# Three bursts of scores in each half batch in place of four, and both value products at the end of odd half batches

## The chip, the cores and the metric

The kernel runs on one core of one Trainium2 chip, all in float32. The metric is the device time of one execution in microseconds. Three runs of the kernel before took 1550.56, 1550.92 and 1552.35 us, so the median is 1550.92 us.

The core's engines are named as the profile names them: TensorE (PE; its weight loads are PEld), VectorE (DVE), ScalarE (ACT), GpSimd (POOL), and SyncE (SP), which here only issues DMAs. [...]

## The reference

The model is one layer: cross-attention of 64 queries over 1601 context keys in 32 batches, then a small attention over the 64 rows with a score that depends on positions, then a feed-forward part with a shared expert and two experts for each row. The cross-attention, cut to what matters:

```python
qh = _split_heads(q @ wq_w.T + wq_b)          # 32 batches, 16 heads of 16, 64 queries
kh = _split_heads(k @ wk_w.T + wk_b)          # 1601 keys
vh = _split_heads(v @ wv_w.T + wv_b)
scores = jnp.einsum('bhqd,bhkd->bhqk', qh, kh) / jnp.sqrt(jnp.float32(D_K))
scores = jnp.where(mask, scores, jnp.float32(-1000000000.0))
attn = jax.nn.softmax(scores, axis=-1)
out = jnp.einsum('bhqk,bhkd->bhqd', attn, vh)
```

The second attention ("span") takes 512 rows of 256 further: `mean = sigmoid(span0) * m`, `soft = softplus(span1)`, `scores = -soft * (pos - mean)**2`, softmax, and a product with the values. Here one tile of it holds 128 rows, that is two batches.

## The kernel before

**Tiling.** The keys of a batch are 13 blocks of 124, the last one padded. The work goes by half batches: half batch n = (b, c) holds batch b and heads 8c to 8c+7, as four pairs of heads j = 0 to 3. There are 64 half batches. For each, `scores` multiplies the transposed keys `kT` by the block-diagonal queries `qbd`. The four pairs j sit in four strips of 32 rows of TensorE, so the four products of one block run side by side, each into its own PSUM bank (psc). VectorE adds the mask (L510) and writes the sum to `prob`; it also takes a running maximum over blocks (`maximum`, L531), block by block, into `mrun` and, with the last block, into `mx`. `turned_maxima` transposes mx on TensorE (pm, L538), `maxima_of_rows` reduces it on VectorE (mc, L545), `maxima_along_rows` spreads it again (pb on TensorE, L553, and the copy mb on ScalarE, L557). GpSimd then subtracts mb from the four pairs (`less_maxima`, L562), ScalarE takes the exponentials (L567), and `values` (pvs, L577) multiplies them with the values, in two calls r = 0 and 1 of two pairs each, in strips of 32 columns.

**Pipeline.** In the step of the main loop for half batch n, the scores of n + 1, a part of the keys (`project_keys`, pk, L456) and values (`project_values`, pv) of batch b + 1, the subtraction and exponentials of n and the value products of n - 1 are all interleaved. The order is written out: a manual schedule holds TensorE, VectorE, ScalarE and GpSimd to the order in which the program issues their instructions; SyncE is left out of it. A key or value projection that is marked tiled also goes in strips of 32 columns; others use the whole array.

**Stretches.** A step of the loop has four stretches g = 0 to 3, one for each burst of scores, for blocks 0-3, 4-6, 7-9 and 10-12 (`GROUPS`); `BETWEEN` says which maxima VectorE takes in each. The context comes in the same four pieces. Into stretch g the loop puts the scores of burst g, the keys of piece g, a unit of values (two blocks), the subtraction of pair g, and the exponential of pair g - 1. The exponential of pair 3 and `values(n - 1, 0)` stand at the start of the next step, and `values(n - 1, 1)` in stretch 0, behind pb.

**The agenda.** What belongs to a tile of two batches is written as generators (`query_steps`, `span_steps`) whose pieces `run(stretch)` puts at the end of a stretch; `WAITS` says how many stretches lie between two pieces (`CLOSE` for the last two tiles). `finish_steps` transposes and divides the value products of a finished batch. The pieces of span_steps, in order: (0) po, the residual and its mean; (1) its normalisation; (2) its transpose tr_h; (3) psp, span and z; (4) an exponential; (5) sixteen small operations on VectorE; (6) a GpSimd subtraction on sc; (7) a square and a GpSimd product on sc; (8) a minimum on VectorE; (9-12) exponentials on ScalarE in four parts; (13) a reciprocal and a GpSimd product on sc; (14) pval; (15) eight transposes psa; (16) po2 (L339); (17) po3 (L349), the residual, its mean and the store x_kept; (18) a normalisation; (19) the transpose tr_f.

**PSUM.** Six banks are shared in turn by everything but two (`mm_bank`): psc, pm, pk, pb, pv and the tiles' products. A new use takes a bank that an earlier user has been read out of. One bank holds pvs and, in its other half, the transposed pvs; one holds mrun.

Of the kernel before, what the change touches and what calls it, by code (L numbers as in the profile page):

```python
# [20 lines left out]
PSUM = bass.MemoryType.PSUM  # L21

# [11 lines left out]
BETWEEN = [(), (1, 2, 3), (4, 5, 6), (7, 8, 9), (10, 11, 12)]  # L34
# [42 lines left out]
def perceiver_kernel(ctx: ExitStack, tc: tile.TileContext, a: dict[str, bass.AP], out: bass.AP):  # L77
# [34 lines left out]
    def load_x(t: int):  # L112
        xs[t] = work.tile([P, D], F32, tag="x", bufs=4, name=f"x{t}")
        nc.sync.dma_start(out=xs[t], in_=a["x"][t * P : (t + 1) * P, :])
# [98 lines left out]
    WAITS = (1, 1, 1, 1, 6, 1, 1, 1, 1, 1, 1, 1, 1, 3, 1, 3, 1, 1, 1)  # L213
    CLOSE = (1, 1, 1, 1, 2, 1, 1, 1, 1, 0, 0, 0, 1, 1, 1, 1, 1, 1, 1)

    SMALL = 5

    def waits_of(t: int):
        return CLOSE if t >= NTILE - 2 else WAITS

    def span_steps(t: int, oT):
        waits = iter(waits_of(t))
# [154 lines left out]


# [6 lines left out]
    def pair_of(n: int, j: int):  # L385
        return prob[:CHUNK, place(n, j // 2), j % 2]
# [15 lines left out]
    nc.vector.memset(pvs, 0.0)  # L402

# [89 lines left out]
    def scores(n: int, g: int, between=(), then=None):  # L493

        b, c = halves[n]
        c0, nb = GROUPS[g]
        pss = [mm_bank(f"psc_{b}_{c}_{g}_{j}") for j in range(4)]
        for k in range(nb):
            for j, ps in enumerate(pss):
                at = (c0 + k) * CHUNK  # L500
                nc.tensor.matmul(  # L501
                    ps[:CHUNK, k * P : (k + 1) * P],
                    lhsT=kTs[c][32 * j : 32 * j + 32, at : at + CHUNK],
                    rhs=qbd[b // 2][32 * j : 32 * j + 32, c, b % 2, :, :],
                    start=True, stop=True, tile_position=(32 * j, 0),
                )
        between = deque(between)
        held = then() if then else None
        for j, ps in enumerate(pss):
            nc.vector.tensor_tensor(  # L510
                pair_of(n, j)[:, c0 : c0 + nb, :].rearrange("p k (e q) -> p k e q", e=2),
                ps[:CHUNK, : nb * P].rearrange("p (k e q) -> p k e q", k=nb, e=2),
                madd[:CHUNK, c0 : c0 + nb, None, :].to_broadcast([CHUNK, nb, 2, S]), ALU.add,
            )
            if between and j:
                maximum(n, between.popleft())
            if j == 1 and held is not None:
                maxima_of_rows(*held)
# [127 lines left out]
    def finish_steps(b: int, stretch: int):  # L646
# [14 lines left out]
        if b % 2:  # L661
            agenda[stretch + 1].append(span_steps(t, oT.pop(t)))
            held_at.add(stretch + 1 + sum(waits_of(t)[:SMALL]))
# [19 lines left out]
    for g in range(len(GROUPS)):  # L683
        scores(0, g, BETWEEN[g])
        if g == 0:
            first_maxima(0)
        project_keys(0, 1, g)
    for k in BETWEEN[-1]:
        maximum(0, k)
# [13 lines left out]
    extra = {4 * last - 4: (0,), 4 * last - 3: (1, 2), 4 * last - 2: (4, 5), 4 * last - 1: (6,)}  # L703
    for n, (b, c) in enumerate(halves[:-1]):
        if c == 0 and b + 1 < B:
            load_context(b + 1)
        if c and b % 2 == 0 and b // 2 + 1 < NTILE:
            agenda[4 * n + 2].append(query_steps(b // 2 + 1))
# [4 lines left out]

        if n:
            values(n - 1, 0)
            exponentials(n - 1, 3)
        for g in range(len(GROUPS)):
            if g == 0:
                turned = []

                def turn():
                    turned.extend(turned_maxima(n))
                    return turned

                scores(n + 1, g, BETWEEN[g], turn)
                project(project_keys, c, 0)
                m = maxima_along_rows(turned[1])
                less_maxima(n, 0, m, nc.gpsimd)
                if 4 * n not in held_at:
                    first_maxima(n + 1)  # L730
                run(4 * n)
                if n:
                    values(n - 1, 1)
                    if c == 0:
                        agenda[4 * n + 1].append(finish_steps(b - 1, 4 * n + 1))
            else:
                scores(n + 1, g, BETWEEN[g])
                project(project_keys, c, g, g == 3)
                if g == 1:
                    project(project_values, 3 * c)  # L740
                elif g == 2:
                    project(project_values, 3 * c + 1)
                else:
                    for u in (5, 6) if c else (2,):
                        project(project_values, u, True)
            if g == 3:
                for k in BETWEEN[-1]:
                    maximum(n + 1, k)
            if g:
                less_maxima(n, g, m, nc.gpsimd)  # L750
                run(4 * n + g)
            for u in extra.get(4 * n + g, ()):
                linear_factor(u)
            if g == 0:
                if 4 * n in held_at:
                    first_maxima(n + 1)
            else:
                exponentials(n, g - 1)


    stretch = 4 * last
# [173 lines left out]
```

## Time and profile before

The profiled execution took 1550.89 us, and the span from its first to its last instruction is 1549.1 us; the clock granted to TensorE was 0.997.

| engine | busy us | share of the span |
|---|---|---|
| TensorE (PE) | 1494.5 | 96% |
| VectorE (DVE) | 1207.5 | 78% |
| GpSimd (POOL) | 1117.2 | 72% |
| ScalarE (ACT) | 953.1 | 62% |
| DMA engines | | 16% (two data queues: 15.5% and 0.2%) |

| work | count | mean ns of one | busy us |
|---|---|---|---|
| scores psc, L501 | 6656 | 284 | 263.4 |
| keys pk, L456 | 1768 | 498 | 404.0 |
| values pv, L456 | 3524 | 379 | 390.9 |
| value products pvs, L577 | 13312 | 220 | 216.4 |
| mask additions of 3 blocks, L510 | 768 | 547 | 404.3 |
| mask additions of 4 blocks, L510 | 256 | 681 | 163.8 |
| running maxima, L531 (without mx) | 704 | 687 | 483.4 |
| subtraction, L562 on GpSimd | 252 | 3741 | 938.9 |
| exponentials, L567 on ScalarE | 256 | 1588 | 403.2 |

A row of the timeline gives the start in us, the length in us, the engine, the line, the operation, output<-inputs, the shape, and in brackets the idle time of the engine before it and who ended it. Matmuls overlap, and a row's length takes in the way through the engine; what one group costs is best read from its start to the start of the next. A row for a matmul counts two instructions for each float32 product.

### The profile page before, as it was taken

To read this page: it belongs to the slowest core of one execution; us is meant where nothing else is said; L and a number is where in the kernel's file an instruction comes from. 1 tells how busy PE (TensorE), PEld (TensorE's weight loads), DVE (VectorE), ACT (ScalarE), POOL (GpSimd) and SP (SyncE) were. 2 spreads that over 40 slices of the span, in tenths; PEclk is the share of its full clock that TensorE was granted. 3 is DMA by queue.
4 is the path that set the end of the run, shared out by engine and by line. 5 is a ranking of instruction groups with operands and counts; after the bars stand their busy time and mean duration, and the time that the engine had idled before them with its cause. 6 is when DMAs were issued, how large, how long until landed. Compare 5 with 4: busy or idle time off the path is not lost.

```text
span 1549.1 us, 61567 instructions
## 1 busy us (share of the span) xinstructions
PE 1494.5 (96%) x27856; PEld 1090.3 (70%) x27856; DVE 1207.5 (78%) x2460; ACT 953.1 (62%) x1725; POOL 1117.2 (72%) x506
## 2 busy tenths in 40 slices
PE   8999999999999999999999999999999999988999
PEld 5677767677777777676767767676777677654587
DVE  4888988878798888888888988888788988884100
ACT  3565676766667666766667566766666676757511
POOL 1777787887778787888777887878877787872610
PEclk9999999999999999999999999999999999999999
DMA  5111111111111111111111111111111111005100
GB/s 169 53 45 44 37 45 36 42 45 52 45 52 46 39 35 39 45 39 51 46 52 46 52 32 42 35 39 48 45 52 45 52 41 33 9 3 161 58 28 28
DMA packets 52070, 73.71 MB, mean 48 GB/s; under 512 B 3812, under 2 KB 51040, under 8 KB 51680
## 3 DMA queue, kind: packets, MB, share of 16 engines
q1 hardware_dynamic: 50992, 69.00, 15.5%
q8 instruction: 218, 3.57, 0.9%
q10 hardware_dynamic: 816, 0.79, 0.2%
q14 instruction: 44, 0.36, 0.1%
HBM read 65.57 MB, written 4.19 MB: 45 GB/s over the span
## 4 chain that ended last, share of the span: by engine, by line
PE 58%; POOL 18%; DVE 18%; ACT 4%; issue 2%; DMA 1%; ACTq 0%; POOLq 0%; DVEq 0%
PE pk L456 14%; POOL prob L562 13%; PE pv L456 12%; PE psc L501 9%; DVE mrun L531 8%; PE pvs L577 8%; DVE prob L510 6%; PE py L865 4%; PE u L606 3%; PE pm L538 2%; PE ph L847 2%; ACT prob L567 2%; POOL sc L289 2%; POOL sc L284 2%; PE pb L553 1%
## 5 line engine op out<-in xcount | busy, mean ns | idle before, releaser
L562 POOL TENSOR_TENSOR prob<-prob,mb 124x1664 f32<-124x1664 f32 x252 | 938.9, 3741 | 270.1 <-ACT mb L557 259.2
L510 DVE TENSOR_TENSOR prob<-psc,madd 124x384 f32<-124x384 f32 (+1 forms) x1024 | 568.1, 580 | 188.8 <-PE psc L501 187.5
L531 DVE TENSOR_TENSOR mrun<-prob,mrun 124x512 f32<-124x512 f32 x704 | 483.4, 687 | 4.4
L567 ACT ACTIVATE prob<-prob 124x1664 f32<-124x1664 f32 x256 | 403.2, 1588 | 44.5 <-POOL prob L562 41.4
L456 PE MATMUL pk<-ct,wkT_sb 128*32 128x361 f32 (+2 forms) x1768 | 404.0, 498 | 7.5 <-DMA wkT_sb<-in_wkT 5.5
L456 PE MATMUL pv<-wvT_sb,ct 128*124 128x256 f32 x3524 | 390.9, 379 | 0.0
L456 PEld LDWEIGHTS pv<-wvT_sb,ct 128*124 128x124 f32 x3524 | 273.4, 132 | 120.1 <-issue 16.3
L501 PE MATMUL psc<-qbd,kT 32*124 32x128 f32 x6656 | 263.4, 284 | 4.5 <-issue 2.3
L471 ACT ACTIVATE kT<-pk,cols 128x372 f32<-128x372 f32 (+2 forms) x256 | 151.6, 592 | 183.3 <-PE pk L456 182.5
L501 PEld LDWEIGHTS psc<-qbd,kT 32*124 32x124 f32 x6656 | 212.5, 181 | 55.2 <-DVE mrun L531 22.8
L488 ACT COPY v<-pv 124x512 f32<-124x512 f32 (+1 forms) x224 | 124.6, 556 | 198.3 <-PE pv L456 198.2
L456 PEld LDWEIGHTS pk<-ct,wkT_sb 128*32 128x32 f32 (+1 forms) x1768 | 158.2, 144 | 116.3 <-issue 51.5
L577 PE MATMUL pvs<-prob,v 124*17 124x64 f32 x13312 | 216.4, 220 | 12.0 <-ACT prob L567 10.3
L577 PEld LDWEIGHTS pvs<-prob,v 124*17 124x17 f32 x13312 | 197.2, 98 | 36.2 <-ACT prob L567 12.7
L296 ACT ACTIVATE sc<-sc,least 128x64 f32<-128x64 f32 x256 | 85.8, 340 | 0.0
L867 DVE SCALAR_TENSOR_TENSOR ot<-py,prob 128x256 f32<-128x256 f32 x16 | 6.8, 424 | 75.7 <-PE py L865 75.7
L523 ACT COPY mrun<-prob 124x512 f32<-124x512 f32 x64 | 38.4, 600 | 40.9 <-DVE soft L279 37.9
L606 PE MATMUL u<-xfT,sw_sb 128*128 128x512 f32 x128 | 57.6, 600 | 0.4 <-ACT xfT L360 0.4
L538 PE MATMUL pm<-cst,mx 124*128 124x124 f32 x256 | 41.1, 282 | 17.3 <-DVE mx L531 16.5
L553 PEld LDWEIGHTS pb<-cst,mc 128*124 128x124 f32 x256 | 29.0, 134 | 39.8 <-DVE mc L545 31.5
L296 ACT ACTIVATION_READ_ACCUMULATOR sc<-sc,least 128x1 f32 x256 | 48.8, 191 | 0.0
L854 ACT ACTIVATE hT<-ph,cols 128x256 f32<-128x256 f32 x32 | 13.4, 470 | 56.3 <-PE ph L847 56.3
(120 smaller groups left out, 1117.0 us busy)
## 6 DMA issues: line engine op xcount, KB each, us to landing
ct<-in_ctxT SPq DMA_DIRECT2D x64, 372.0 KB, 3.2
ct<-in_ctxT SPq DMA_DIRECT2D x32, 496.0 KB, 3.6
ct<-in_ctxT SPq DMA_DIRECT2D x32, 361.0 KB, 3.2
w<-in_w SPq DMA_DIRECT2D x16, 256.0 KB, 6.9
x<-in_x SPq DMA_DIRECT2D x16, 128.0 KB, 2.4
x_kept<-x SPq DMA_DIRECT2D x16, 128.0 KB, 1.7
prob<-x_kept SPq DMA_DIRECT2D x8, 256.0 KB, 4.9
out<-ot SPq DMA_DIRECT2D x16, 128.0 KB, 1.9
```

Source lines behind the costliest of these rows:

```text
L296: nc.scalar.activation(sc[:, h, :], sc[:, h, :], AF.Exp, bias=least[:, h : h + 1], scale=-1.0, accum_out=total[:, h : h + 1],)
L456: nc.tensor.matmul(out[at:end], lhsT=lhsT[:, at:end], rhs=rhs, start=start, stop=stop, **(dict(tile_position=(0, at)) if tiled else {}),)
L471: nc.scalar.activation(kTs[c][:, k0 : k0 + kn], ps[:, :kn], AF.Identity, bias=cols[:, B_K + c : B_K + c + 1])
L488: nc.scalar.copy(vs[b % 2][:kn, 2 * u : 2 * u + n, :, :DK], ps[:kn, : n * D].rearrange("p (n h d) -> p n h d", n=n, d=DK),)
L501: nc.tensor.matmul(ps[:CHUNK, k * P : (k + 1) * P], lhsT=kTs[c][32 * j : 32 * j + 32, at : at + CHUNK], rhs=qbd[b // 2][32 * j : 32 * j + ...
L510: nc.vector.tensor_tensor(pair_of(n, j)[:, c0 : c0 + nb, :].rearrange("p k (e q) -> p k e q", e=2), ps[:CHUNK, : nb * P].rearrange("p (k e ...
L531: nc.vector.tensor_tensor(dst, block_of(n, k), run, ALU.max)
L538: nc.tensor.transpose(ps[:, j * CHUNK : (j + 1) * CHUNK], m[:CHUNK, j, :], ident[:CHUNK, :CHUNK])
L562: engine.tensor_tensor(sj, sj, m[:CHUNK, j, None, :].to_broadcast([CHUNK, NKC, P]), ALU.subtract)
L567: nc.scalar.activation(pair_of(n, j), pair_of(n, j), AF.Exp)
L577: nc.tensor.matmul(pvs[32 * j : 32 * j + DK + 1, c, :, r, :], lhsT=v[:kn, k, 8 * c + h, :], rhs=pair_of(n, h // 2)[:kn, k, (h % 2) * S : ( ...
L606: nc.tensor.matmul(ps, lhsT=w[:, c, hc * P : (hc + 1) * P], rhs=xfT[:, c, :, slot], start=(c == 0), stop=(c == 1),)
```

## The change

The half batch now has three stretches, with scores of 4, 5 and 4 blocks (`SCORED`). A fifth block doesn't fit a bank that holds four, so the four fifth products go to two more banks: one from the six (`more[0]`, for pairs 0 and 2) and the half of the pvs bank that holds the transposed pvs (`more[1]`, for pairs 1 and 3). [...] VectorE adds the mask to the fifth blocks in two operations A and B, with a doubled copy of the mask, `madd_fifth`, that GpSimd makes once. The order of additions (0-3, A, B), maxima (m1 to m12) and the row reduction (t) on VectorE is written out in `ORDER`.

The context still comes in four pieces. Keys of piece 0 stand in stretch 0, of piece 1 in stretch 1, of pieces 2 and 3 in stretch 2, both in strips. Values are two units in stretch 1 and one in strips in stretch 2; odd half batches have a further one in stretch 0. `values(n - 1, 1)` stays behind pb in even half batches and moves to the end of the step in odd ones, where `values(n, 0)` of the next step follows it. The exponential of pair 0 stands behind the scores of stretch 1, of pair 1 at the end of stretch 1, of pair 2 in stretch 2 between the two key pieces; the subtraction of pair 2 is issued ahead of the scores of stretch 2, that of pair 3 behind the values of stretch 2.

The agenda counts three stretches a half batch, and `STEPS` gives the place of each piece. With A, B, C, D for n mod 4 = 0, 1, 2, 3 and the stretch behind it, the pieces of span_steps fall so. Before: 0 in A2, 1 A3, 2 B0, 3 B1, 4 B2, 5 D0, 6 D1, 7 D2, 8 D3, 9-12 A0-A3, 13 B0, 14 B3, 15 C0, 16 C3, 17 D0, 18 D1, 19 D2, where "A" after D is the next cycle. After: 0 in B0, 1 B1, 2 C0, 3 C1, 4 C2, 5 D0, 6 D1, 7 D2, 8 and 9 B0, 10 B1, 11 B2, 12 C0, 13 C1, 14 C2, 15 D0, 16 D2, 17 A1, 18 A2, 19 B0. The query's steps begin in B1 (before: B2) and take one stretch each; finish_steps stands in stretch 1 of A and C in both. The pool for x has five buffers in place of four. The prelude for half batch 0 has three bursts as well.

```diff
+SCORED = [(0, 4), (4, 5), (9, 4)]
+ORDER = [
+    "0 1 t 2 3",
+    "A 0 m1 1 m2 B 2 m3 3 m8 m4 m5",
+    "0 1 m6 2 m7 3 m9 m10 m11 m12",
+]
...
-    WAITS = (1, 1, 1, 1, 6, 1, 1, 1, 1, 1, 1, 1, 1, 3, 1, 3, 1, 1, 1)
-    CLOSE = (1, 1, 1, 1, 2, 1, 1, 1, 1, 0, 0, 0, 1, 1, 1, 1, 1, 1, 1)
+    STEPS = (3, 4, 6, 7, 8, 9, 10, 11, 15, 15, 16, 17, 18, 19, 20, 21, 23, 25, 26, 27)
...
+        more = [mm_bank(f"psc_{b}_{c}_{g}"), spare_pvs] if nb == 5 else None
         pss = [mm_bank(f"psc_{b}_{c}_{g}_{j}") for j in range(4)]
+        for r in range(nb):
+            for j in range(4):
+                e, s = divmod(j, 2)[::-1]
+                fifth = nb == 5 and r == 4 * s
+                i = 4 if fifth else r - (nb == 5 and s == 0)
+                ps, at = (more[e], s) if fifth else (pss[j], i)
+                if fifth and j == 2:
+                    tc.add_manual_dep(nc.tensor.nop().ins, mm.ins.name, IN_TURN, reason="banks")
...
+        scores(n + 1, 0, taken_off)
+        project(project_keys, c, 0)
+        m = maxima_along_rows(turned[1])
+        less_maxima(n, 0, m, nc.gpsimd)
+        held = 3 * n in held_at
+        if not held:
+            first_maxima(n + 1)
+        if c:
+            project(project_values, 3)
+        run(3 * n)
+        if n and c == 0:
+            values(n - 1, 1)
+            agenda[3 * n + 1].append(finish_steps(b - 1, 3 * n + 1))
...
+        scores(n + 1, 1)
+        exponentials(n, 0)
+        project(project_keys, c, 1)
+        for u in (4, 5) if c else (0, 1):
+            project(project_values, u)
+        less_maxima(n, 1, m, nc.gpsimd)
+        steps(1)
+        exponentials(n, 1)
+
+        less_maxima(n, 2, m, nc.gpsimd)
+        scores(n + 1, 2)
+        project(project_keys, c, 2, True)
+        exponentials(n, 2)
+        project(project_keys, c, 3, True)
+        project(project_values, 6 if c else 2, True)
+        less_maxima(n, 3, m, nc.gpsimd)
+        steps(2)
+        if c:
+            values(n - 1, 1)
```

## The prediction

> **What bounds the kernel now.** I read the engines' shares first, then the waits, then the order of time through one half batch.
>
> ```profile
> PE 1494.5 (96%) x27856; PEld 1090.3 (70%) x27856; DVE 1207.5 (78%) x2460; ACT 953.1 (62%) x1725; POOL 1117.2 (72%) x506
> ```
>
> TensorE is busy for 96% of the span, so its own work sets the pace, and what it still waits for is the rest. The list of waits (waiter, releaser: us in total, times, longest) shows on whom:
>
> ```profile
> POOL prob L562 <- ACT mb L557: 259.2, 61, 10.4
> ...
> PEld psc L501 <- DVE mrun L531: 22.8, 67, 0.8
> ...
> PE pm L538 <- DVE mx L531: 16.5, 19, 2.0
> ...
> PE pvs L577 <- ACT prob L567: 10.3, 14, 1.0
> ```
>
> GpSimd has 259.2 us of slack, about 4 us a half batch, always before the first subtraction (L562). TensorE's waits are for VectorE's last maximum (mx) and for late exponentials. The timeline of one half batch, TensorE and then VectorE (start us, length, operation), shows the first of these:
>
> ```profile
> 723.29 0.94 PE L501 MATMUL psc<-qbd,kT 32*124 32x128 f32 x24
> 724.15 1.52 PE L456 MATMUL pk<-ct,wkT_sb 128*128 128x372 f32 x4
> 725.50 1.89 PE L456 MATMUL pv<-wvT_sb,ct 128*124 128x256 f32 x8
> 727.33 0.94 PE L501 MATMUL psc<-qbd,kT 32*124 32x128 f32 x24
> ...
> 737.73 1.15 PE L501 MATMUL psc<-qbd,kT 32*124 32x128 f32 x32
> 739.77 0.64 PE L538 MATMUL pm<-cst,mx 124*128 124x124 f32 x4 [0.89 <-DVE mx L531]
> ```
>
> ```profile
> 724.24 1.02 DVE L510 TENSOR_TENSOR prob<-psc,madd 124x384 f32<-124x384 f32 x2 [2.92 <-PE psc L501]
> 725.18 0.69 DVE L531 TENSOR_TENSOR mrun<-prob,mrun 124x512 f32<-124x512 f32 x1
> ...
> 733.72 0.18 DVE L186 BATCH_NORM_AGGREGATE mv_h<-stats_h 128x2 f32<-128x6 f32 x1
> ...
> 736.85 2.14 DVE L531 TENSOR_TENSOR mrun<-prob,mrun 124x512 f32<-124x512 f32 x3
> 739.02 0.69 DVE L531 TENSOR_TENSOR mx<-prob,mrun 124x512 f32<-124x512 f32 x1
> ```
>
> From 724.24, 0.09 us after the second burst, VectorE never stops until mx at 739.71, and pm starts 0.06 us later. So there are two tracks between a half batch's second burst and the next pm: TensorE's list, and VectorE's chain. I call half batches A, B, C, D by n mod 4 = 0, 1, 2, 3. From pm at 674.83 to pm at 760.90 a cycle of four takes 86.1 us: C 21.8, D 21.2, A 21.9, B 21.1. Comparing each group of matmuls there with the shortest of its kind gives 3.1 us of waits (A 2.1, C 0.55, D 0.5); 83.0 us is TensorE's work.
>
> **The change: what TensorE saves.** Costs are from start to start of rows.
> Scores: a burst of 3 blocks takes 0.864, of 4 takes 1.082 (each as 724.15 - 723.29), so a block is 0.218 and a burst's fixed part 0.21. Before, 1.082 + 3 x 0.864 = 3.674; after, 1.082 + 1.300 + 1.082 = 3.464: 0.21 saved a half batch.
> Keys: one piece fewer follows a burst whole (1.354) and goes in strips (1.276, the strip row's 1.238 for 361 columns scaled to 372); the last piece no longer follows a burst (1.21): 0.105 saved.
> Value projection next to a burst is 1.820, next to itself 1.727: 0.093 saved in A and C.
> Value products in odd half batches: between whole-array products they cost 1.579, plus 0.14 on the pb ahead. Among strips no row shows them followed by more strips: between 1.45 (their own streaming rate to the end) and 1.568 (followed by a burst); I take 1.46, since no switch follows: 0.26 saved in B and D.
> A cycle saves 4 x 0.315 + 2 x 0.093 + 2 x 0.26 = 1.97 us, which leaves 81.0: A 19.3, B 20.2, C 21.1, D 20.4.
>
> **The fifth block's wait.** The nop waits for a matmul of the same burst. [...] I take 0 and keep 13 for the range.
>
> **VectorE.** Before, 12 additions of 384 at 0.468 and 4 of 512 at 0.598; after, 12 of 512 and two of 256 (no row; 0.34 on the line through 384 and 512, between 0.2 and 0.468). Per half batch about 0.3 less, but its place is what counts. A maximum after another maximum starts 0.73 later, after an addition 0.595. So the middle order is 0.34 x 2 + 0.598 x 4 + 0.595 x 4 + 0.73 x 2 = 6.9 us, the last one (to the end of mx, 0.72 for the maximum after addition 3) 6.6 us.
>
> **The steps that move.** They cost the same instructions, but in new places, and each stands in in-order queues. Three now bring a VectorE result that GpSimd needs into stretch 1, behind the whole 6.9 us of the middle order: po3's residual and mean in A (1.0 us), the query's mean in B (0.55), the sum of span and its reciprocal in C (0.66). GpSimd has them between the second and the third subtraction, so the third and fourth wait too. Behind the third stands its exponential on ScalarE, and, new in this order, behind that exponential the copies of the last key piece and the last values, which free their PSUM banks. The banks are what TensorE needs for the next scores and pm. Before, the copy of the last keys stood behind the exponential of the second subtraction, and a mean was ready by the time that GpSimd came to it (mv_h at 733.90 above; GpSimd's rows, where three subtractions end at 733.88):
>
> ```profile
> 722.78 11.10 POOL L562 TENSOR_TENSOR prob<-prob,mb 124x1664 f32<-124x1664 f32 x3 [2.74 <-ACT mb L557]
> 733.99 0.22 POOL L188 TENSOR_SCALAR rstd_h<-mv_h 128x1 f32<-128x1 f32 x1
> ...
> 735.19 3.75 POOL L562 TENSOR_TENSOR prob<-prob,mb 124x1664 f32<-124x1664 f32 x1
> ```
>
> The other steps find cover: the sixteen small operations of VectorE in D (2.9 us) and least in B (1.1) lie in stretch 0, where it idles from 3.1 to the second burst's end; the store of x_kept goes with po3 behind the context pieces on SyncE's queue, where nothing waits for it but an x load, which has five buffers now, and the DMA engines are 15% busy.
>
> Laid out from pm = 0, with a subtraction 3.68, an exponential 1.58, a copy of keys 0.56:
> **A.** Second burst ends at 0.48 + 1.67 + 0.53 + 1.58 + 1.30 = 5.56. VectorE from 5.65: 6.94 + 1.0 + 1.29 (finishing the batch) + 6.58 = 21.47. The next pm is at 21.5: 2.2 of waiting.
> **B.** Burst ends at 0.48 + 1.67 + 0.44 + 1.73 + 0.86 (po) + 0.31 + 1.30 = 6.79. The mean is ready at 6.88 + 6.94 + 0.55 = 14.4. GpSimd starts here at 3.55 (A's mean at 13.6 puts A's fourth exponential 2.3 into B, ahead of the copy of mb) and is idle from 3.55 + 2 x 3.68 + 1.2 = 12.1. Then 1.2 + 3.68: third subtraction done at 19.3, exponential 20.9, key copy 21.45. At pm all six banks are taken, four by scores not yet read, and pm has to wait for that copy: 21.5, against 20.2 of work.
> **C.** B's fourth subtraction ends at 23.0, ScalarE is busy with the tile's steps to 23.5, so the fourth exponential ends at 25.1, here 3.6, and the value products wait 0.45; the burst, which needs five of six banks, waits 0.3 for the copy of tr_h. It ends at 6.85. VectorE: 6.94 + 6.94 + 0.66 = 14.55. GpSimd: 1.9 + 3.68, 20.15. Exponential 21.75, key copy 22.3. TensorE would reach the next scores at 20.75, but pk, pv and pval hold three banks, all behind that exponential; the fourth score bank comes at 22.3: 1.55 lost. C takes 23.3.
> **D.** The burst waits 0.45 for the copy behind psa; 20.85.
> Sum 87.2 against 86.1: **the saving of 1.97 is eaten by 3.1 more of waits**, +1.1 a cycle. From n = 4 to 61 there are 14.5 cycles: +16 us. Ahead of these are some five half batches without tile steps, which save about 0.4 each: -2. Before the loop one burst goes, at its end the steps keep their spacing to within a stretch: 0, give or take 3. Together +14. The one extra copy on GpSimd and the fifth x buffer cost nothing, under the first loads. The profiled execution took 1550.89, and the median is 1550.92, so the sum gives **1565 us**.
>
> **Rivals.** (1) *The waits don't grow* and TensorE keeps its saving: 14.5 x 1.97 + 2 = 31 us, **1520 us**. For it: GpSimd's 259 us of slack, which could take the delay. Its mechanism is that the key copy's bank is not what the next burst needs. It decides from the point where 1.1 of the 3.1 us of new waits goes, for instance if C's scores found a fourth bank at 20.75. Against it: three tiles and five or six banks leave no room in the count. (2) *VectorE alone bounds*: without the bank waits, A stays at 21.5, B falls to 21.0, C to 22.5 (14.55 + 1.29 + 6.58), D 20.85: 85.9, so about 3 to 5 us faster, **1546 us**. For it: today's waits are VectorE's. (3) *The nop drains*, or banks are also short at the third burst in B and D, where the fourth score bank is added up only at 11.75, when TensorE comes at 11.7: up to 13 + 7 us more, **1583 us**. (4) That nothing changes would need the waits to cancel the saving just so.
>
> **Chances and range.** The layout as summed 0.60, rival 3 0.13, rival 2 0.15, rival 1 0.12. A difference of 0.2% (3 us) is what a measurement can tell. Rival 1 and two thirds of rival 2 are faster: 0.22; the rest of rival 2 and a little of the main case are within: 0.08; slower 0.70. The main case's own range is 1554 to 1577 (half a microsecond a cycle either way and the ends). The whole range takes in rival 2 and most of rival 3, 1537 to 1587, and leaves out rival 1 and the worst of 3.
>
> **What would show it.** Right: scores rows of x40 taking 1.30; TensorE's busy sum lower; GpSimd's rstd_q, rstd_f and sc waiting for VectorE in the list of waits; psc waiting for ACT kT or prob once in four half batches; cycles near 87. Wrong: cycles near 84 (rival 1), pm waiting only for mx (rival 2), or a gap in the middle of each x40 row (rival 3). The forecast falls if ScalarE's key copy comes before the third exponential, or if GpSimd reaches the third subtraction by 12 in B and C.

## The result, and the profile after

The changed kernel takes 1631.37 us (median of four runs, 1627.31 to 1632.62) against 1551.63 us before (1550.56 to 1552.79). The ratio is 1.0509, with an interval of 1.0488 to 1.053: some 80 us slower, where the forecast was 14 us slower with a range that ended at 1587. The direction was right, the size was not.

The profiled execution of the changed kernel has a span of 1625.5 us, and the clock granted to TensorE is 0.985 (before: 1549.1 us and 0.997). The engines' line of its page:

```profile
PE 1500.5 (92%) x27856; PEld 1101.6 (68%) x27856; DVE 1217.6 (75%) x2332; ACT 943.5 (58%) x1725; POOL 1118.6 (69%) x508
```

TensorE is busy for 92% of the span where it was 96%, and its busy sum hasn't fallen, though a half batch now does less. The list of waits (waiter, releaser: us in total, times, longest) had these rows before:

```profile
ACT prob L567 <- POOL prob L562: 41.4, 17, 3.1
...
PE psc L501 <- issue: 2.3, 6, 0.7
...
PE pvs L577 <- issue: 1.7, 3, 0.8
```

Now it has large rows for TensorE, and rows for GpSimd that were forecast:

```profile
ACT prob L606 <- POOL prob L601: 311.3, 170, 4.7
...
POOL rstd_f L197 <- DVE mv_f L195: 58.8, 15, 16.9
...
POOL sc L314 <- DVE total L313: 44.9, 16, 7.1
PE pvs L616 <- issue: 40.4, 24, 3.1
POOL rstd_q L197 <- DVE mv_q L195: 39.3, 16, 4.3
...
PE psc L529 <- ACT kT L490: 22.5, 27, 1.5
...
PE psc L529 <- issue: 13.7, 9, 2.0
...
PE pm L577 <- DVE mx L570: 7.0, 5, 2.4
```

The three GpSimd rows, the exponentials behind GpSimd (41.4 us before, 311.3 now) and the scores waiting for the key copy (`kT`) are the prediction's chain. The two rows with "issue" are not in it: TensorE stands, and nothing that the profile shows holds it. Before, such stops of over 0.4 us came to 3.1 us in all (5 of them); now they come to 54.7 us (34). The timeline of TensorE at the end of a D shows one (start us, length, operation, and in brackets the idle time ahead of it):

```profile
748.35 2.40 PE L616 MATMUL pvs<-prob,v 124*17 124x64 f32 x155
753.23 1.28 PE L616 MATMUL pvs<-prob,v 124*17 124x64 f32 x53 [2.48 <-issue]
754.44 2.08 PE L529 MATMUL psc<-qbd,kT 32*124 32x128 f32 x32
756.45 0.95 PE L577 MATMUL pm<-cst,mx 124*128 124x124 f32 x4
```

The two value products are 208 matmuls in a row. After 155 of them TensorE stops for 2.48 us. Then the burst of 32 scores takes 2.01 us from start to start, not 1.08. The reason for that is in the windows of the same stretch, whose columns are the busy time and count of each engine, then the granted clock (PEclk), the DMA share and GB/s:

```profile
752.00:754.00 2.00, 0.77 (x48) 0.77 (x50) 0.18 (x1) 1.60 (x2) 2.00 (x2) 0.93 0.00 0
754.00:756.00 2.00, 2.00 (x45) 1.80 (x40) 0.00 (x0) 0.00 (x0) 0.02 (x1) 0.50 0.03 8
756.00:758.00 2.00, 2.00 (x18) 1.40 (x12) 1.39 (x3) 0.00 (x0) 0.00 (x0) 0.72 0.00 0
```

After the stop the clock is at half for 3.41 us. The changed kernel has ten such half-speed periods in its loop and before has none; over the whole execution (period by one minus its clock, summed) they are worth 23.9 us against 5.0. They lengthen TensorE's rows (the burst above took 2.01 us in place of 1.08), which I take for most of the reason why its busy sum didn't fall.

For A the forecast order of VectorE is there nearly to the tenth. These are VectorE's rows between pm at 663.60 and pm at 685.52, and GpSimd's row that waits for them:

```profile
669.27 0.42 DVE L546 TENSOR_TENSOR prob<-psc,madd_fifth 124x256 f32<-124x256 f32 x1 [2.46 <-PE pvs L529]
...
677.10 0.18 DVE L195 BATCH_NORM_AGGREGATE mv_f<-stats_f 128x2 f32<-128x6 f32 x1
...
684.33 0.69 DVE L570 TENSOR_TENSOR mx<-prob,mrun 124x512 f32<-124x512 f32 x1
```

```profile
677.37 0.23 POOL L197 TENSOR_SCALAR rstd_f<-mv_f 128x1 f32<-128x1 f32 x1 [2.79 <-DVE mv_f L195]
```

VectorE starts 5.67 us after pm (forecast 5.65), its mean is ready at 13.68 (13.6), mx ends at 21.42 (21.47). But mx isn't what holds the next pm, as the layout had it: pm comes 0.50 later, because the burst ahead of it waited for the key copy.

```profile
684.45 1.14 PE L529 MATMUL psc<-qbd,kT 32*124 32x128 f32 x26 [1.47 <-ACT kT L490]
```

The table has the mean time from pm to pm over the ten cycles from the 16th half batch on. "Work" is the sum over the groups of matmuls, each taken at the shortest of its kind in that trace.

| | before | forecast | after | work before | work after |
|---|---|---|---|---|---|
| A | 21.95 | 21.5 | 21.95 | 19.72 | 19.23 |
| B | 21.20 | 21.5 | 22.59 | 21.08 | 20.33 |
| C | 21.89 | 23.3 | 23.35 | 21.19 | 21.02 |
| D | 21.22 | 20.85 | 23.27 | 20.70 | 20.57 |
| cycle | 86.26 | 87.2 | 91.16 | 82.69 | 81.14 |

The work fell by 1.55 us a cycle (forecast: 1.97). The rest of the cycle, waits and slower clock together, grew from 3.6 to 10.0, not to 6.2. C is as laid out, A is 0.45 above, and the miss is B, by 1.1 us, and D, by 2.4. In these ten cycles the stops come to 1.5 us in the mean B and 2.2 in the mean D, nearly as much as the 4 us by which the cycle is over its forecast. Some of what was laid out isn't there: of the wait of pm for the key copy in B, put at 1.3 us, 0.13 is left.

### The profile page after: what moved, and what is told of

It reads as the page before. It is cut to its first block, busy times and chain, and to the rows that moved or that the text cites. A ratio compares the mean times of both kernels' runs of the same rounds, so it can differ in the third digit from the quotient of the medians.

```text
span 1625.5 us, 61499 instructions
## 1 busy us (share of the span) xinstructions
PE 1500.5 (92%) x27856; PEld 1101.6 (68%) x27856; DVE 1217.6 (75%) x2332; ACT 943.5 (58%) x1725; POOL 1118.6 (69%) x508
## 4 chain that ended last, share of the span: by engine, by line
PE 54%; DVE 16%; POOL 16%; ACT 6%; issue 6%; DMA 0%; POOLq 0%; ACTq 0%; DVEq 0%
POOL prob L601 13%; PE pk L475 13%; PE pv L475 11%; PE psc L529 10%; DVE mrun L570 8%; PE pvs L616 7%; DVE prob L553 5%; PE py L909 3%; ACT prob L606 3%; PE u L645 2%; PE pm L577 2%; PE ph L891 2%; POOL sc L314 2%; PE pb L592 1%; ACT kT L490 1%
## 5 line engine op out<-in xcount | busy, mean ns | idle before, releaser
L606 ACT ACTIVATE prob<-prob 124x1664 f32<-124x1664 f32 x256 | 407.3, 1591 | 314.0 <-POOL prob L601 311.3
L553 DVE TENSOR_TENSOR prob<-psc,madd 124x512 f32<-124x512 f32 x768 | 506.7, 680 | 95.4 <-PE psc L529 93.9
L475 PE MATMUL pk<-ct,wkT_sb 128*32 128x372 f32 (+1 forms) x2512 | 398.6, 494 | 13.0 <-ACT qbd L454 7.2
L475 PE MATMUL pv<-wvT_sb,ct 128*32 128x256 f32 (+1 forms) x2780 | 386.3, 380 | 7.3 <-DVE prob L553 7.3
L475 PEld LDWEIGHTS pv<-wvT_sb,ct 128*32 128x32 f32 (+1 forms) x2780 | 284.0, 145 | 103.9 <-DVE prob L553 24.4
L529 PE MATMUL psc<-qbd,kT 32*124 32x128 f32 x6400 | 259.2, 284 | 37.7 <-ACT kT L490 22.5
L475 PEld LDWEIGHTS pk<-ct,wkT_sb 128*32 128x32 f32 (+1 forms) x2512 | 152.7, 128 | 148.6 <-issue 95.7
L546 DVE TENSOR_TENSOR prob<-psc,madd_fifth 124x256 f32<-124x256 f32 x64 | 27.2, 425 | 127.3 <-PE pvs L529 121.3
L314 POOL TENSOR_TENSOR sc<-sc,total 128x1024 f32<-128x1024 f32 x16 | 30.4, 1902 | 44.9 <-DVE total L313 44.9
L529 PE MATMUL pvs<-qbd,kT 32*124 32x128 f32 x256 | 55.0, 293 | 0.6 <-issue 0.6
```

The source lines that it names most:

```text
L475: nc.tensor.matmul(out[at:end], lhsT=lhsT[:, at:end], rhs=rhs, start=start, stop=stop, **(dict(tile_position=(0, at)) if tiled else {}),)
L529: product = nc.tensor.matmul(ps[:CHUNK, at * P : (at + 1) * P], lhsT=kTs[c][32 * j : 32 * j + 32, k0 : k0 + CHUNK], rhs=qbd[b // 2][32 * j ...
L553: nc.vector.tensor_tensor(pair_of(n, j)[:, c0 : c0 + 4, :].rearrange("p k (e q) -> p k e q", e=2), pss[j][:CHUNK].rearrange("p (k e q) -> ...
L606: nc.scalar.activation(pair_of(n, j), pair_of(n, j), AF.Exp)
```

## The experiments

Three suspects: the stops in the value products (instructions that come too late), the copies behind the third exponential (banks), and VectorE's chain. Each kernel is an edit of the changed one unless it says before, and computes the whole reference. "Stops" are TensorE's idle times of over 0.4 us that have no cause in the trace.

**Product back behind pb.** In odd half batches too:

```diff
-        if n and c == 0:
+        if n:
             values(n - 1, 1)
+        if n and c == 0:
             agenda[3 * n + 1].append(finish_steps(b - 1, 3 * n + 1))
...
-        if c:
-            values(n - 1, 1)
```

> The changed kernel with one part undone: in odd half batches the second value product stands behind pb again. Instruction theory (TensorE uses up its instructions in the 416 of two value products in a row, and stands until the next block of 256 has come): the 55 us of standing for nothing that the profile shows go, and some 8 us of switching come back: 1584 us (1572 to 1595). Bank theory (the prediction's: what is lost is waiting for copies behind late exponentials): nothing is won, 8 us of switching come back: 1630 to 1645 us.

Measured: 1645.35 us, ratio 1.0601 (1.0579 to 1.0623). Stops fell to 6.7 us and D to 21.9, as the theory of instructions has it, and still the kernel is 14 us slower than the changed one. Its waits:

```profile
PE pm L577 <- ACT kT L490: 35.0, 15, 2.4
PE psc L529 <- ACT kT L490: 25.2, 29, 1.9
```

With the product ahead of the second burst, VectorE's first addition of that burst comes 8.49 us after pm in B, not 7.04, and 10.2 where a half-speed period falls on it (five of the ten cycles); the mean, the third exponential and the key copy come later with it. Together these two rows are 60.2 us, where the changed kernel has 22.5 and 1.3. The half-speed periods are worth 49.4 us. So -48 of stops, +36 of waits for the key copy and +25 of clock, which comes near the +14 measured: the number that the bank theory named came out, but by a wait that replaced the stops, not because the stops were harmless.

**Before, with that one part of the change.** values(n - 1, 1) of odd half batches goes to the end of the step:

```diff
-                if n:
+                if n and c == 0:
                     values(n - 1, 1)
...
+        if c:
+            values(n - 1, 1)
```

> The kernel before with that part alone: four bursts, but in odd half batches the second value product at the end of the step, next to the first of the next step. Instruction theory: the same standing appears here, some 1.7 us in each of 31 odd half batches, less 8 us of switching and less the waits for late exponentials at pb: 1585 us (1570 to 1600). Bank theory: no bank is held longer, so the switching is saved: 1535 to 1550 us.

Measured: 1618.57 us, ratio 1.0444 (1.0417 to 1.0471), without any of the other parts. Stops 46.8 us:

```profile
PE pvs L577 <- issue: 34.3, 24, 2.7
```

B goes to 23.1 and D to 24.65. Where no stop falls into them, the two products take 3.02 us, the 1.45 and 1.57 that the prediction reckoned with. The price of the products was right; what it leaves out is the stops. Not all of the 67 us are stops, though: the half-speed periods cost 11 us more than before, and the last run of this section shows a part of the rest.

**Products apart.** values(n - 1, 1) stands between the third and the fourth key piece:

```diff
         project(project_keys, c, 2, True)
+        if c:
+            values(n - 1, 1)
         exponentials(n, 2)
         project(project_keys, c, 3, True)
...
-        if c:
-            values(n - 1, 1)
```

> The changed kernel, with values(n-1, 1) of odd half batches taken from the end of the step to between the third and fourth piece of the keys, so that the two value products no longer stand in a row (the next step's first product is about 3 us of whole keys and values away) and neither stands ahead of a burst that VectorE's chain waits for. If TensorE starves for instructions where 208 small products follow each other, the gaps with no cause in the trace fall from 54.7 us to under 12, and the time goes to 1631 - 45 = 1586 us (1578 to 1596). If those gaps go with the number of value products and not with their standing together, they stay and the time is 1625 to 1640. If the clock's half-speed windows take the gain back, as with the product ahead of the burst, the gaps fall, the granted clock falls to 0.97, and the time is 1605 to 1630.

Measured: 1594.81 us, ratio 1.0289 (1.0257 to 1.032); stops 15.5 us, clock 0.988. That is 36.6 us less than the changed kernel for 39.2 us less of stops. In this place the product takes 1.46 us.

**One unit of values between them.** The same two lines stand ahead of `project(project_values, 6 if c else 2, True)`, so 32 instructions and 0.86 us lie between the products:

```diff
         project(project_keys, c, 3, True)
+        if c:
+            values(n - 1, 1)
         project(project_values, 6 if c else 2, True)
```

> The changed kernel with values(n-1, 1) of odd half batches ahead of the last unit of values in strips, so that 0.86 us of matmuls (32 instructions) stand between the two value products, where the changed kernel has none and the run with the products apart 2.1 us. In the trace of the changed kernel TensorE stops when some 512 instructions are used since the fetch before, and goes on 2.3 us after the next fetch starts. If it is the rate of instructions that starves it, the gaps of 54.7 us fall by the 0.86 us that each of 30 stalls is given, to 25 to 35 us, and the time is 1604 to 1614. If the gaps come from two value products next to each other as such (the same PSUM bank, strips of the same kind), they fall to the 15 us of the run with the products apart: 1590 to 1600. If they are tied to the number of fetches only: 1625 to 1632.

Measured: 1595.57 us, ratio 1.028 (1.0262 to 1.0298); stops 22.8 us. The stops went from 34 of 1.61 us in the mean to 26 of 0.88: 0.73 less each, for 0.86 us of other work. The stops are just under the 25 to 35 us named for a rate, the time is that of the products apart, so this run can't tell a rate from mere neighbourhood. What can is where the stops fall. I numbered TensorE's instructions in the trace of the changed kernel (matmuls, weight loads, and the 332 waits and drains of its sequencer), and took the first one behind each stop; fetches are the 16 KB packets of queue 8, which the page calls instruction; I take them for TensorE's because there are 219 of them for its 56044 instructions, one for each 256:

```
goes on   stood   number of the instruction   last fetch began
 753.23    2.48    27329 = 106 x 256 + 193     2.36 us earlier
 843.86    0.64    30657 = 119 x 256 + 193     2.39
 847.34    1.06    30913 = 120 x 256 + 193     2.30
 936.33    2.71    34241 = 133 x 256 + 193     2.33
1252.69    3.10    46273 = 180 x 256 + 193     2.49
```

All 34 stops of the changed kernel are at 256 k + 193, and so are all 5 of before and every one in the thirteen kernels of this section: 269 of 269. I read this as a block of 256 run to its last instruction, with TensorE standing for the next; it goes on 2.2 to 3.1 us after that fetch began. Two value products are 416 instructions in 3.0 us; at that pace a block lasts 1.9 us. In the changed kernel a fetch begins 0.7 us (the median of 200; from 2.9 us ahead to 3.8 us behind) after TensorE has gone over to the block before; with 2.2 us or more behind that, I estimate that a block which lasts under some 3 us can be caught out.

**Copies first.** The third exponential goes behind the copies of the last keys and values:

```diff
         project(project_keys, c, 2, True)
-        exponentials(n, 2)
         project(project_keys, c, 3, True)
         project(project_values, 6 if c else 2, True)
+        exponentials(n, 2)
```

> The changed kernel with the third exponential behind the copies of the last keys and values on ScalarE, so that these banks come free without it. If both theories hold, the waits of scores and pm for these copies go (22 us in the list of waits, and up to 10 of pk behind them) and the standing for instructions stays: 1605 us (1595 to 1618). If late copies cost nothing beside the instructions: 1625 to 1635 us. If they are all of it, as the prediction had it: 1560 us.

Measured: 1609.06 us, ratio 1.0369 (1.0352 to 1.0385). The scores' waits for the key copy are gone from the list, C fell from 23.35 to 22.5, the stops stayed at 50.1 us.

**Third subtraction first.** It is issued ahead of the tile's steps of the second stretch, so GpSimd doesn't hold it for VectorE's mean:

```diff
         less_maxima(n, 1, m, nc.gpsimd)
+        less_maxima(n, 2, m, nc.gpsimd)
         steps(1)
         exponentials(n, 1)
-        less_maxima(n, 2, m, nc.gpsimd)
```

> The changed kernel with GpSimd's third subtraction ahead of the tile's steps of stretch 1, so that it no longer waits for VectorE's mean or reciprocal there. Both theories: the third exponential comes 2 to 3 us earlier in three of four half batches and the copies behind it too: 1608 us (1598 to 1620), standing for instructions unchanged near 55 us. Instruction theory alone: 1625 to 1638 us.

Measured: 1611.65 us, ratio 1.039 (1.0373 to 1.0408), stops 56.9 us. The row rstd_f <- mv_f is down to 22.1 us in 2 waits. Two different cuts of the same chain, on ScalarE and on GpSimd, give 22 and 20 us: the chain of the prediction is real. After either, A's pm waits for mx as laid out (A 21.55 and 21.58).

**Products apart and copies first, together.** Both edits above.

> The changed kernel with the value products apart, as in the run before, and the third exponential behind the copies of the last keys and values. If starvation and the late copies are two separate losses, both gains add: 1586 - 22 = 1564 us (1552 to 1575), with no wait of scores for the key copy left and waits of pm for VectorE's last maximum in their place. If the late copies only cost something where TensorE was already late, this is the run before, 1586.

Measured: 1565.98 us, ratio 1.0107 (1.0082 to 1.0133), clock 0.996. The gains more than add: 36.6 us, and 28.8 where the copies alone gave 22. What TensorE now waits for is VectorE's last maximum:

```profile
PE pm L577 <- DVE mx L570: 28.7, 28, 2.4
```

A takes 21.47, B 21.23, C 22.51, D 21.50. That is near the prediction's rival 2, VectorE alone (21.5, 21.0, 22.5, 20.85), but for D, where 0.4 us of stops are left.

**Product behind pb, copies first.** The first edit with the exponential moved.

> The changed kernel with values(n-1, 1) behind pb in all half batches, and the third exponential behind the copies of the last keys and values. The product behind pb alone gave 1645 us. If its loss was that the later second burst made the third exponential, and behind it the key copy, late, then 60 us of waits for that copy go, the waits of pm for VectorE's last maximum take a part of their place, and the time is 1585 to 1605. If its loss was the half-speed windows of the clock or VectorE's chain itself, it stays at 1630 to 1645.

Measured: 1598.79 us, ratio 1.0314 (1.0297 to 1.0331). The 47 us that it gained over the first run confirm what had hidden the stops' removal there. It is 33 us behind the run before, with stops of 4.7 us: with the second burst 1.45 us later in B and D, VectorE's chain ends later (pm waits 67.4 us for mx). So the move of the value product does help VectorE, provided that it isn't put beside the other.

**All three.** Products apart, copies first, third subtraction first.

> The changed kernel with the value products apart, the third exponential behind the copies, and the third subtraction ahead of the tile's steps of the second stretch. If the mean, the sum and the query's mean that GpSimd waits for cost time only through the exponential and the copies behind it, this adds nothing to the run before: 1560 to 1566 us. If they also delay the last exponential and with it the value products of the next step, a further 5 to 10 us go: 1555. Below 1549 would mean that the three bursts do bring their 0.5 us a half batch once the three losses are gone.

Measured: 1559.1 us, ratio 1.0043 (1.0027 to 1.0059), with the same wait for mx, 30.0 us, so a gain of 7 us over the two edits. That fits the second of the two expectations, within 4 us: GpSimd's waits for the mean and the sum cost something beyond the third exponential. Through which instruction was not isolated.

**The agenda alone.** po3's mean behind the last stretch of A, the sum's reciprocal and GpSimd's product behind the last of C, psa behind the second of D, the query's mean in the first of B:

```diff
-    STEPS = (3, 4, 6, 7, 8, 9, 10, 11, 15, 15, 16, 17, 18, 19, 20, 21, 23, 25, 26, 27)
+    STEPS = (3, 4, 6, 7, 8, 9, 10, 11, 15, 15, 16, 17, 18, 20, 20, 22, 23, 26, 27, 28)
...
-            agenda[3 * n + 1].append(query_steps(b // 2 + 1))
+            agenda[3 * n].append(query_steps(b // 2 + 1))
```

> The changed kernel with the agenda alone edited: po3 with its residual and mean behind the last stretch of A (not the second), the reciprocal of the sum and GpSimd's product with it behind the last of C, the transposes psa behind the second of D, the query's mean in the first stretch of B; so nothing of a tile that GpSimd needs from VectorE lies behind the 6.9 us of the middle order, and VectorE has 2.2 us less between a cycle's second bursts and its last maxima. If the moved steps cost what the prediction laid out, the waits of GpSimd for mv_f, mv_q and total almost go, the waits of scores for the key copy with them, and some 20 to 30 us are gained: 1600 to 1612 us, with the 50 us of starvation still there. If the starvation alone is the loss: 1625 to 1633.

Measured: 1614.56 us, ratio 1.0424 (1.0394 to 1.0453). The gain of 17 us is a little under the range that was named. A fell to 20.84 and the waits of scores for the key copy to 1.1 us, but the rows of GpSimd didn't go as expected: only rstd_q's wait fell (39.3 to 4.2 us), sc's grew to 53.3, and rstd_f still waits 63.4, now behind the fourth subtraction, where the next half batch's first one isn't due yet. The stops, 54.1 us, stayed, and B grew to 24.2.

**Everything cleared.** Products apart, copies first, and this agenda.

> The changed kernel with the value products apart, the copies ahead of the third exponential, and the agenda of the run before. With the products apart and the copies first the time was 1566 us, with A at 21.48 (VectorE's chain as the prediction laid it out, 21.47), B 21.2 and C 22.3 between pm and pm. If VectorE's chain is what bounds A, B and C there, it is 1.0, 0.5 and 0.66 shorter now: 16 tiles by 2.2 are 35 us at most, and with TensorE's own work below it (19.3, 20.2, 21.1) close behind, 1532 to 1545 us, below the kernel before. If instead TensorE's own work or GpSimd's chain is next in line at once, 1555 to 1566.

Measured: 1551.91 us, ratio 1.0007 (0.9997 to 1.0017), the level of before and not the gain that was expected. Its engines' line and TensorE's largest wait:

```profile
PE 1480.6 (96%) x27856; PEld 1076.9 (70%) x27856; DVE 1212.3 (78%) x2332; ACT 950.3 (61%) x1725; POOL 1119.8 (72%) x508
```

```profile
PE pm L577 <- DVE mx L570: 19.6, 31, 2.4
```

TensorE's busy sum is 13.9 us below before, and 96% again. A fell to 20.74 and C to 22.10, but B rose to 21.79 (21.23 with the products apart and the copies first): po3's mean now stands on VectorE right behind mx, so mc behind pm waits for it and pb for mc, 0.4 us. The cycle is 85.9 (before: 86.3), and from the last pm to the last instruction 162.7 us pass where before took 157.5.

**po3's mean one step later.** On top of the kernel with everything cleared, to take that wait away: the residual stays behind mx, the mean goes to the first stretch of B, the transpose tr_f to the last (in the last three tiles the agenda moves a little too):

```diff
-        spread = spread_of(x, f"f{t}")
         nc.sync.dma_start(out=x_kept[t], in_=x)
+        yield next(waits)
+        spread = spread_of(x, f"f{t}")
```

> The kernel with everything cleared (1551.9 us), with the mean of po3's residual no longer right behind VectorE's last maximum of A but in the first stretch of B, so that the reduction mc behind pm doesn't wait for it, and po3 of the last tile but two a stretch sooner. If what kept the cleared kernel from a gain is VectorE's order around pm, B (21.5 to 22.0) goes to 21.0 to 21.4, which is 0.5 us in 14 cycles and 7 us, and the tail loses 2 of the 5 us that it had over the kernel before: 1541 to 1547 us, below the kernel before. If B is bound by TensorE's own work or by the exponentials by then: 1549 to 1553.

Measured: 1586.09 us, ratio 1.0229 (1.0215 to 1.0243), a clear miss. B takes 24.6. GpSimd's rows in a B of this kernel:

```profile
928.38 3.72 POOL L602 TENSOR_TENSOR prob<-prob,mb 124x1664 f32<-124x1664 f32 x1 [5.72 <-ACT mb L597]
932.18 0.23 POOL L197 TENSOR_SCALAR rstd_h<-mv_h 128x1 f32<-128x1 f32 x1
...
933.51 0.21 POOL L197 TENSOR_SCALAR rstd_f<-mv_f 128x1 f32<-128x1 f32 x1
...
934.81 0.22 POOL L197 TENSOR_SCALAR rstd_q<-mv_q 128x1 f32<-128x1 f32 x1
...
936.02 7.46 POOL L602 TENSOR_TENSOR prob<-prob,mb 124x1664 f32<-124x1664 f32 x2
```

Three normalisations now stand between the first two subtractions and hold the second for 3.84 us. The transpose tr_f, new in the last stretch, has its copy (xfT) at 948.92, behind a late exponential and eight small operations of the tile; pm waits for that bank:

```profile
PE pm L578 <- ACT xfT L373: 14.0, 9, 1.6
```

I moved a step by VectorE's clock and didn't count its GpSimd and ScalarE instructions, in the stretch where two others stood already.

**Before, product apart.** In the kernel before the same product goes between the last keys and the values in strips:

```diff
+                    if c:
+                        values(n - 1, 1)
                     for u in (5, 6) if c else (2,):
                         project(project_values, u, True)
```

> The kernel before with one part of the change alone, but without its value products in a row: values(n-1, 1) of odd half batches leaves its place behind pb and goes into the last stretch, between the last keys and the two units of values, 2.6 us of matmuls ahead of the next value product. The same move to the very end of the step had cost 67 us, with 47 us of gaps without a cause. If those gaps are all that was wrong with it, B and D keep near 21.1 us, C 21.9, and A shows the 20.7 that it had there (21.9 before), since the second burst comes 1.6 us sooner in D and all behind it with it: 1.0 to 1.3 us a cycle less and 1533 to 1545 us, below the kernel before. If the move itself is bad (late value products, clock), 1555 to 1580.

Measured: 1561.64 us, ratio 1.0063 (1.0051 to 1.0076), 0.6% slower than before and in the range named for a move that is bad in itself, with stops of only 4.5 us. A showed the 20.76 that was expected, but D went from 21.22 to 22.96: there a group of keys is 0.8 and a burst of scores 0.7 longer than the shortest of their kind. Weight loads of scores wait for VectorE's mask additions 49 times and 16.7 us in all (before: 16 times, 6.1 us). Another wait is new, that of values for the bank that VectorE's residual of po3 frees (none before):

```profile
PE pv L456 <- DVE x L352: 7.4, 12, 0.7
```

The timelines show what holds VectorE. In D its sixteen small operations and that residual stand in the first stretch, ahead of the second burst's additions. In the D that starts at 699.34 the first of those additions comes 7.09 us after pm, and in the kernel before (D at 696.63) 7.09 as well: with the product out of the way TensorE has the second burst done 1.6 us sooner, and VectorE isn't ready for it. Behind pb the product stood where TensorE had to wait for VectorE anyway; in its new place its 1.46 us come on top, which fits D's 1.7. So even without stops the move by itself brings the kernel before nothing. The kernel with that product at the end of the step has both waits too (16.7 and 7.7 us), so they are in its 67 us.

## Why the prediction was wrong in size

- **The savings on TensorE** held. A burst of five takes 1.300 us at its shortest, with rounds of 0.218 throughout, as worked out. The work of a cycle fell by 1.55 us, 0.4 less than the sum of 1.97.
- **A slip that changes nothing**: from the costs given for VectorE's additions, a half batch goes from 8.01 to 7.86 us, which is 0.15 less and not "about 0.3"; the layout doesn't use it.
- **The nop** costs nothing, as taken. It stands in the last round of a burst of five, ahead of the fifth products of pairs 2 and 3, and waits for that of pair 1, four rounds of 0.218 us earlier. The last round starts 0.218 us after the one ahead of it, as the others do, and in all 64 bursts of five its two halves are 0.11 to 0.12 us apart. So no run shows the 13 us kept for the range and in rival 3; what the runs show is a burst of 1.300 us without a drain.
- **VectorE's orders** came out at 6.92 us (669.27 to 676.19) and 6.56 (678.46 to mx's end at 685.02), forecast 6.9 and 6.6. C follows the layout. A's number nearly did, by another path: the layout has pm waiting for mx, but the key copy held the burst ahead of pm (1.42 us in the mean A), a bank wait that it had in B and C alone.
- **The chain of the moved steps** (VectorE's mean, GpSimd, third exponential, key copy, bank) is shown by the runs that cut it at ScalarE and at GpSimd, 22 and 20 us. With the stops out of the way the cut is worth 29.
- **The step that failed** is the value products: "Among strips no row shows them followed by more strips ... I take 1.46, since no switch follows: 0.26 saved in B and D". That costs the 208 matmuls of two products in a row by their streaming rate and takes for granted that 416 instructions can always be had in 3 us. Here they often could not: stops of 54.7 us, of which the runs with the products apart took away 39 and gained 37 us. D was laid out at 20.85 with no wait but 0.45; it measured 23.27, with 1.93 of the excess in the value products.
- **What the sum had no line for** is the clock. Half-speed periods cost 18.9 us more than before. Of the ten in the changed kernel's loop, nine start between 0.6 us ahead of and 1.6 us behind the end of a stop of 1.50 to 3.10 us, and the tenth, at 685.46, 1.01 us behind the wait of 1.47 us for the key copy. In the run that cleared both the clock was 0.996, so I take this for a price on top of stops and waits and not a separate cause. In one of the ten B it is all of the excess ahead of the second burst: VectorE gets to that burst 8.67 us after pm at 685.52, where it is 7.04 in the other nine (laid out: 6.88), and from 685.5 to 688.9 the granted clock is 0.50.
- **The end** was put at 0, give or take 3. From the last pm to the last instruction the changed kernel takes 162.6 us, before 157.5.
- **No rival** named stops: rival 3's 1583, the nearest to 1631, rests mostly on a drain that isn't there. **Rival 1** (1520 us, the saving kept) stays refuted even with all three losses cleared, where pm waits for VectorE's mx again. The kernels in that state, at 1552 to 1566, are nearest to rival 2 (1546).

The three clearings in turn, 36.6 us for the products, 28.8 for the copies, 14.1 for the agenda, make up the 80 us and end level with the kernel before. That leaves open in part why no version ends below it. Shown is that pm still waits for mx (19.6 us), that the end is 5 us longer, and that the one attempt on what VectorE has between mx and mc opened another wait.

## What to carry to other kernels

Cost a run of small matmuls by its count of instructions (a weight load counts as one) as well as by its time, and keep a group of longer ones between two such runs: here 208 instructions in 1.5 us mostly went unnoticed, and 416 in 3 us cost 55 us in stops. When a step moves, lay out the queue of every engine that it touches in the new place, since here the third exponential ahead of a key copy cost 22 to 29 us, and the run with three normalisations between two subtractions was 34 us slower. Take a stop away and look at once at what comes late next: the first repair here removed 48 us of stops and made the kernel 14 us slower.

## What the runs showed of the hardware

All 269 stops of over 0.4 us in the fifteen kernels are at an instruction of number 256 k + 193, and TensorE goes on 2.2 to 3.1 us after the start of a 16 KB packet of queue 8 that itself takes 0.9 to 1.7 us. That TensorE's instructions come in blocks of 256, and that a block is not always there in time, is my reading of these numbers. One value product by itself (208 instructions) nearly went without stops (5 of them, 3.1 us, before); two in a row (416) did not (34, 54.7 us). Why some fetches only start when the block in hand is used up, as at 750.87 us, 0.12 us after TensorE stopped, the trace doesn't show.

Of the twelve half-speed periods in the changed kernel's span, ten lasted 3.41 us and two 6.83. The length of a stop alone doesn't tell whether one follows: a stop of 1.50 us, ending at 800.38, was followed by half speed from 801.51 on, and one of 2.71 us, ending at 936.33, was not.
